# First image of a conv-attention kernel: column sums of the exp tiles taken by TensorE into a held PSUM bank, and the key maps' small levels moved to another buffer and convolved first

## The chip, the cores and the metric

The kernel runs on one core of one Trainium2 chip. The metric is the device time of one launch in microseconds (us), in float32 throughout. Three runs of the kernel before took 3240.96, 3236.12 and 3240.89 us; the median is 3240.89 us. One further execution was taken by the hardware profiler; its own time stands in the table below.

## The reference, cut to what matters

Input `x` is 8 images of 256 channels and 32x32 pixels. The network is a convolutional attention layer, then a token attention layer, then eight gated experts. Only the first layer is touched.

```python
# layer 0, per image; C = 256, HEADS = 8, DH = 32
q = einsum('bchw,oc->bohw', x, q_w)                    # 1024 queries per head
k_map, v_map = kv[:, :C], kv[:, C:]                    # kv = kv_w applied to x
def pooled(t):                                         # four levels: 32x32, 16x16, 11x11, 5x5
    for i, r in enumerate([1, 2, 3, 6]):
        p = average_pool(t, r)
        p = p + depthwise3x3(p, dconv_w[i], dconv_b[i])
        outs.append(p.reshape(B, C, -1))
    return concatenate(outs, axis=2)                   # 1024 + 256 + 121 + 25 = 1426 keys
ks_ = layernorm(pooled(k_map).T); vs_ = layernorm(pooled(v_map).T)
attn = softmax(einsum('bhqd,bhkd->bhqk', q, k) * SCALE)   # over the 1426 keys
out_att = einsum('bhqk,bhkd->bhqd', attn, v)
```

The softmax needs, for every head and query, the sum of the exponentials over all 1426 keys.

## The kernel before, in words

**Stages.** `attention` (line 913) computes layer 0 and layer 1 of all images, interleaved; `experts` follows. The main loop of `attention` walks over images b, head groups c (four heads each), halves of the queries, and key chunks kc of 128 keys. One (b, c, half) is called a unit here; a unit has 11 full chunks, and image 0 has units 0 to 3. The chunks of a unit come in the order 0 to 7, then 11 (once per image), then 8 to 10.

**One step of the loop.** `scores` (1509) makes four products with 32 contracted rows each into one tile `sc` of four PSUM banks; ScalarE takes the exponential of the tile into `pt` (128 x 2048, six buffers). One step later `values` (1519) multiplies the four heads' parts of `pt` with the value tokens `vt` into the bank `pv`. Chunk 11 has only 18 keys: `tail_scores` (1531) puts its exponentials, for all four units of an image, into the tile `ptail`, which is allocated at line 1083 and not used before that.

**The sums.** Every second exp tile is added into the one before it by an accumulating DMA that GpSimd issues (`add`, 1564), so a unit yields six "pairs"; the sixth also gets its rows of `ptail` (`tail_add`, 1556). The generator `sums` (1571) then adds pairs 1 to 5 into pair 0 on VectorE, two instructions of 128 x 1024 each, ten a unit, and at the end sums pair 0 over its partitions by four products with a block of ones. `normalise` (1590) takes the reciprocal and scales the attention output.

**PSUM.** A partition has eight banks: four for `sc`, one for `pv`, two for `sm` and one for `sx`. `small()` (929) hands out one of the last three for all work beside the loop.

**The maps of image 0.** `first_maps` (1172) projects the four maps (0 and 1 keys, 2 and 3 values) and copies them out of PSUM; the key maps' copies `p` lie in two of the six `pt` buffers, the value maps' copies in `p0` and `p1`. The 32x32 level of the keys is convolved on TensorE (`first_keys`, 1220), all other levels by `taps` (1243), eight multiply-adds on VectorE per level and map. `first_taps` (1257) does the values' large level, then the small levels of maps 2, 3, 0, 1 in this order. The small keys of map 0 are the buffer `kn`, those of map 1 the buffer `v`, the values `acc`. `key_tokens` (1473) and `value_tokens` (1460) turn finished maps into normalised tokens, in three groups of four chunks; the third group needs the small levels.

**What sets the order.** Every instruction goes through class `Flow`, whose helper at line 670 records it: so all lines of the profile say L670. `Flow` keeps its own estimate of each engine's time and lays down one fixed order for each engine. Side work is a set of generators with ranks, which yield what they need next; between two steps of the loop `step` (882) resumes those that `runnable` (855) lets through. A TensorE request is let through only if its data are expected 1.5 us before the next scores may start, and only against a credit for each step. `finish(cond)` (895) resumes generators until the condition holds, whatever the loop would do next. The loop calls it, among others, before the fifth step of image 0 (line 1917), where it waits until the small levels of both key maps are done, and before the values products of a chunk whose group of `vt` is not there (line 1934). On the chip each engine then works its order off and waits on semaphores.

**Side work named below.** `mix` and `weights1` prepare the weights of the output projection and of layer 1 (tiles `gw`, `bnvec`, `res`, `p`); `convolve` (1270) does image 1 onwards.

Of the kernel before, what the change touches and what calls it, by code (L numbers as in the profile page):

```python
# [10 lines left out]
AF = mybir.ActivationFunctionType  # L11
# [5 lines left out]
P = 128  # L17
C = 256
HW = 1024
HEADS = 8  # L20
DH = 32
# [3 lines left out]
NKC = 12  # L25
# [11 lines left out]
NEAR = {"DVE": 1.5, "ACT": 2.0, "POOL": 1.0, "SP": 10.0}  # L37
BUFS = {"sm": 2, "sx": 1}
AHEAD3 = 3
PACE2 = 8.0  # L40
NBOUND = 64
NSTAGED = 64
# [870 lines left out]
def attention(tc, kit, f, outer, ended, nb, consts, x, t1, t2, hn, bounds, vecs, q_t, kv_t, proj_t, gqk_t, wqk, wqkv, vecs1, w1_d, w1c, gate_d, wrc, vecs2, bnvec):  # L913
# [6 lines left out]
    with ExitStack() as ctx:  # L920
        l1, shared = outer
        wp = ctx.enter_context(tc.tile_pool(name="w0", bufs=1))
        work = ctx.enter_context(tc.tile_pool(name="work0", bufs=1))
        psum = ctx.enter_context(tc.tile_pool(name="psum0", bufs=1, space=PSUM))

        def T(pool, shape, tag, bufs=1):
            return f.tile(pool, shape, tag, bufs=bufs)
# [51 lines left out]
        hi, lo = bounds  # L979
        for t in bounds:  # L980
            f.pool.memset(t, 0.0)
        column = [4 * (n // 4 * 2) + n % 4 for n in range(4 * nb)]
# [98 lines left out]

        ks, qs, vts = {}, {}, {}
        ptail = T(work, [P, 4, 512], "ptail")
        vz = [T(work, [P, P], f"vz{i}") for i in range(2)]
        for t in vz:
            f.pool.memset(t, 0.0)
# [2 lines left out]
        todo, done, read, freed, key_parts, normalised = [], [], [2], [0], [0], [0]  # L1089

        def pe(*tiles, tag=None):
            return "PE", tiles, tag
# [13 lines left out]
        def until(cond):  # L1106
            return None, cond, None
# [50 lines left out]
        first, large, whole, pooled, asked = {}, [], [], [], []  # L1158
# [13 lines left out]
        def first_maps(xp):  # L1172


            for m in range(4):
                if m < 2:
                    p = T(work, [P, 4, 512], "pt", bufs=6).rearrange("p j q -> p (j q)")
                    acc = T(l1, [P, NK], "v") if m else T(work, [P, NK], "kn", bufs=3)
                else:
                    p = pmaps[m - 2]  # L1180
                    acc = T(work, [P, NK], "acc", bufs=3)
                for t in (p, acc):
                    if t is not p or m < 2:
                        f.split(t, 512, HW)
                first[m] = p, acc
            for m, s0 in [(m, s0) for g in (0, 2) for s0 in (0, 512) for m in (g, g + 1)] + [(m, HW) for m in range(4)]:
                if s0 == HW:
                    yield until(lambda: pooled)
                w = min(512, NK - s0)
                c = m % 2  # L1190
                p, acc = first[m]
                src = source(xp, s0, w)
                yield pe(src, tag="sm")
                ps = small()
                for k in range(2):
                    f.pe.matmul(
                        ps[:, :w],
                        lhsT=kvw[:, k, m * P : (m + 1) * P],
                        rhs=src[:, k, :],
                        start=k == 0,  # L1200
                        stop=k == 1,
                    )
                f.act.activation(p[:, s0 : s0 + w], ps[:, :w], AF.Copy)
                for s, n in enumerate(SIDES):
                    a, z = max(OFFS[s], s0), min(OFFS[s] + n * n, s0 + w)
                    if a < z and (m >= 2 or s):
                        f.act.activation(
                            acc[:, a:z],
                            ps[:, a - s0 : z - s0],
                            AF.Identity,  # L1210
                            bias=db(c, s),
                            scale=mid[:, c * 4 + s : c * 4 + s + 1],
                        )
                if (m, s0) == (3, 512):
                    large.append("maps")
                    f.spawn(first_keys(0), 1)
                    f.spawn(first_keys(1), 5)
            whole.append("maps")
# [21 lines left out]
                f.act.activation(acc[:, half * 512 : half * 512 + 512], ps, AF.Identity, bias=db(m, 0))  # L1240
            large.append(("keys", half))

        def taps(c, s, p, acc):
            n, o = SIDES[s], OFFS[s]
            pin = p[:, o : o + n * n].rearrange("p (h w) -> p h w", h=n)
            pout = acc[:, o : o + n * n].rearrange("p (h w) -> p h w", h=n)
            for tap in range(9):
                if tap == 4:
                    continue
                dy, dx, y0, y1, x0, x1 = windows(tap, n)  # L1250
                o_ap = pout[:, y0:y1, x0:x1]
                yield ve(pin[:, y0 + dy : y1 + dy, x0 + dx : x1 + dx], o_ap)
                f.ve.scalar_tensor_tensor(
                    o_ap, pin[:, y0 + dy : y1 + dy, x0 + dx : x1 + dx], dw(c, s, tap), o_ap, ALU.mult, ALU.add
                )

        def first_taps():
            for m in (2, 3):
                yield until(lambda: "maps" in large)
                yield from taps(m - 2, 0, *first[m])  # L1260
                large.append(("values", m))
                read[0] += 1
            yield until(lambda: whole)
            for m in (2, 3, 0, 1):
                for s in range(1, 4):
                    yield from taps(m % 2, s, *first[m])
                whole.append(m)
            done.extend(first[m][1] for m in (2, 3, 0, 1))

# [300 lines left out]

        def sums(n, pairs):

            for i in range(1, NKC // 2):
                yield until(lambda: len(pairs) > i)
                for j in range(0, 4, 2):
                    s = pairs[0][:, j : j + 2, :]
                    yield ve(s, pairs[i])
                    f.ve.tensor_tensor(s, s, pairs[i][:, j : j + 2, :], ALU.add)
            yield until(lambda: normalised[0] == n)
            yield pe(pairs[0], tag="sm")  # L1580
            total = small()
            for j in range(4):
                f.pe.matmul(
                    total[DH * j : DH * j + DH, :], lhsT=kit.ones[:, :DH], rhs=pairs[0][:, j, :], start=True, stop=True
                )
            rec = T(work, [P, 512], "rec")
            f.act.activation(rec, total, AF.Copy, accum_out=hi[:, column[n] : column[n] + 1])
            return rec
# [315 lines left out]
        for i in range(len(steps) + 1):  # L1904
            if i < len(steps):
                b, c, half, kc = steps[i]
                sl = slice(half * 512, half * 512 + 512)
                if kc % 4 == 0:
                    f.finish(lambda: key_parts[0] > 3 * b + kc // 4)
                if (half, kc) == (0, 0):  # L1910
                    f.finish(lambda: (b, c) in qs and (b or (c, 0) in asked))
                    turn[0] = 2 * b + c
                    atts[b, c] = T(work, [P, HW], "att", bufs=2)
                if kc == NKC // 2 and b < nb - 1:
                    f.sp.dma_start(t1[b][:, c, sl], x[b, c * P : (c + 1) * P, sl])
                if i == 4:
                    f.finish(lambda: {0, 1}.issubset(whole))
                if b == 0 and kc == 0:
                    f.finish(lambda: (c, half) in asked)
                if kc == NKC - 1:  # L1920
                    f.finish(lambda: key_parts[0] > 3 * b + 2 and (b, 1) in qs and (b or len(asked) == 4))
                    tail_scores(b)
                else:
                    pts[i] = scores(b, c, sl, kc)
                f.step()
            if i and steps[i - 1][3] < NKC - 1:
                b1, c1, half1, kc1 = steps[i - 1]
                if kc1 == 0:
                    pv = T(psum, [P, 512], "pv")
                    pairs = []  # L1930
                    sl1 = slice(half1 * 512, half1 * 512 + 512)
                    f.spawn(unit(b1, c1, sl1, units, pairs), 0)
                    units += 1
                f.finish(lambda: kc1 // 4 in vts[b1])
                values(b1, c1, kc1, pts[i - 1], pv)
                if kc1 % 2:
                    add(kc1, pts.pop(i - 1), pts[i - 2])
                    pairs.append(pts.pop(i - 2))
                if kc1 == NKC - 2:
                    u = 2 * c1 + half1  # L1940
                    tail_values(b1, u, pv)
                    pairs.append(pts.pop(i - 1))
                    tail_add(u, pairs[-1])
                    f.finish(lambda: projected[0] >= b1)
                    f.act.activation(atts[b1, c1][:, sl1], pv, AF.Copy)
            if i < len(steps):
                f.step((PACE, PACE1))
# [687 lines left out]
```

## Time and profile before

| what | us or share |
|---|---|
| median of three runs | 3240.89 |
| the profiled execution's own time | 3236.82 |
| its span, first to last instruction | 3235.0 |
| mean granted TensorE clock | 0.989 |
| busy: PE (TensorE matmul) | 3064.9, 95% |
| busy: DVE (VectorE) | 2458.7, 76% |
| busy: ACT (ScalarE) | 1692.2, 52% |
| busy: POOL (GpSimd) | 1198.6, 37% |
| ends of image 0's four units (copy of `pv`) | at 185.4, 224.9, 268.5, 311.8 |
| ends of image 1's first two units | at 374.9, 414.3 |
| end of the last unit | at 1856.7 |

Times of the table's last three rows are from the start of the span. A row of the profile's timeline gives start, duration, engine, line, operation, output and inputs, shapes, and in brackets how long the engine had been idle before and which instruction released it. TensorE's rows count two records for each float32 product with 32 columns or rows. PE is short for TensorE, PEclk for the clock that it was granted.

### The profile page before, as it was taken

The numbers are of one execution on the slowest core, as the hardware profiler recorded it, in microseconds if no ns is written. First come the engines' busy times: TensorE is split into PE (matmuls) and PEld (weight loads), VectorE is DVE, ScalarE is ACT, GpSimd is POOL, SyncE is SP. The second block draws the span as 40 slices with busy tenths as digits, with TensorE's granted clock in tenths as the row PEclk, the third lists the DMA queues.
The fourth block names the chain that finished last, engine by engine and source line by source line (L and its number), as shares of the span: only waits on it lengthen the run. The fifth ranks groups of instructions, "written<-read, shape, count | busy, mean of one in ns | idle before, by whom it ended". The sixth has DMA issues, their size and how long they took to land.

```text
span 3235.0 us, 55827 instructions
## 1 busy us (share of the span) xinstructions
PE 3064.9 (95%) x22342; PEld 1793.5 (55%) x22342; DVE 2458.7 (76%) x4064; ACT 1692.2 (52%) x2302; POOL 1198.6 (37%) x1293
## 2 busy tenths in 40 slices
PE   8787899999999999989999999999999999999998
PEld 3422234334334334333433367777888888888887
DVE  5787787987898889988754546346888788777776
ACT  3476676576657666676665523334333333444443
POOL 2312314214232232241111210006756666777775
PEclk9799999999999999999999999999999999999999
DMA  1277656665665565764676653124444442000000
GB/s 51 72 157 169 133 115 146 142 138 122 132 152 121 128 144 120 172 144 88 152 161 128 154 205 134 55 90 163 150 143 150 150 163 72 20 30 23 20 14 21
DMA packets 117196, 375.49 MB, mean 116 GB/s; under 512 B 14512, under 2 KB 40440, under 8 KB 93696
## 3 DMA queue, kind: packets, MB, share of 16 engines
q0 software_dynamic: 28608, 179.85, 28.7%
q1 hardware_dynamic: 84960, 190.01, 17.3%
q8 instruction: 178, 2.92, 0.4%
q10 hardware_dynamic: 3360, 1.97, 0.2%
q14 instruction: 90, 0.74, 0.1%
HBM read 118.74 MB, written 87.60 MB: 64 GB/s over the span
## 4 chain that ended last, share of the span: by engine, by line
PE 71%; DVE 10%; ACT 7%; DMA 4%; issue 4%; POOL 2%; ACTq 0%; DVEq 0%; POOLq 0%; SPq 0%
PE bank L670 22%; PE sm L670 17%; PE y L670 10%; PE sc L670 8%; PE sx L670 8%; PE pv L670 6%; ACT pt L670 5%; DMA pt<-pt 3%; DVE acc L670 3%; DVE rec L670 1%; DVE pt L670 1%; DVE h L670 1%; DMA pt<-ptail 1%; DVE c L670 1%; DVE u L670 1%
## 5 line engine op out<-in xcount | busy, mean ns | idle before, releaser
L670 ACT ACTIVATE pt<-sc 128x2048 f32<-128x2048 f32 x352 | 660.7, 1877 | 269.3 <-PE sc L670 226.8
L670 DVE SCALAR_TENSOR_TENSOR acc<-p,vec,acc 128x961 f32<-128x961 f32 (+3 forms) x960 | 554.9, 586 | 32.0 <-ACT acc L670 6.4
L670 PE MATMUL sc<-q,kn 32*128 32x512 f32 (+1 forms) x3072 | 417.3, 644 | 102.0 <-ACT pt L670 97.9
L670 DVE TENSOR_TENSOR pt<-pt,pt 128x1024 f32<-128x1024 f32 x320 | 388.1, 1260 | 125.6 <-DMA pt<-pt 110.4
L670 PE MATMUL pv<-pt,vt 128*32 128x512 f32 x2816 | 380.1, 612 | 0.1
L670 ACT ACTIVATE p1c<-bank 128x256 f32<-128x256 f32 x226 | 86.6, 383 | 556.2 <-PE bank L670 550.2
L670 ACT ACTIVATE h<-h,bnvec 128x512 f32<-128x512 f32 x452 | 341.9, 805 | 62.7 <-DVE h L670 52.6
L670 POOL DMA_DIRECT2D pt<-pt x160 | 146.1, 913 | 561.2 <-ACT pt L670 438.5
L670 POOL TENSOR_TENSOR rstd<-rstd,mhalf 128x4 f32<-128x4 f32 (+2 forms) x88 | 107.5, 1222 | 624.1 <-DVE rstd L670 592.4
L670 DVE TENSOR_TENSOR h<-p1c,bank 128x512 f32<-128x512 f32 x226 | 154.1, 682 | 222.9 <-PE bank L670 216.0
L670 PEld LDWEIGHTS sc<-q,kn 32*128 32x128 f32 (+1 forms) x3072 | 113.6, 178 | 293.4 <-ACT pt L670 195.8
L670 POOL TENSOR_TENSOR tm<-h,tm 128x256 f32<-128x256 f32 x202 | 234.7, 1162 | 15.8
L670 DVE TENSOR_TENSOR h<-u,bank 128x256 f32<-128x256 f32 x452 | 230.2, 550 | 7.8
L670 PEld LDWEIGHTS pv<-pt,vt 128*32 128x32 f32 x2816 | 55.6, 108 | 271.8 <-issue 257.1
L670 PE MATMUL bank<-h,w2e 128*128 128x256 f32 (+1 forms) x620 | 203.6, 457 | 2.8 <-DVE h L670 1.9
L670 POOL TENSOR_TENSOR tm<-h 128x512 f32<-128x512 f32 x101 | 131.8, 1304 | 189.6 <-ACT h L670 189.6
L670 DVE TENSOR_TENSOR h<-h,gate 128x1024 f32<-128x1024 f32 x128 | 199.6, 1560 | 0.5 <-ACT h L670 0.5
L670 PE MATMUL y<-t,s3e 128*128 128x256 f32 x768 | 187.0, 379 | 1.9 <-POOL t L670 1.7
L670 PE MATMUL bank<-t,s1e 128*128 128x256 f32 x750 | 182.5, 379 | 0.2 <-DVE h L670 0.2
L670 POOL TENSOR_TENSOR t<-h 128x512 f32<-128x512 f32 x104 | 135.0, 1298 | 110.3 <-DVE h L670 93.3
L670 PE MATMUL sm<-y,t 128*32 128x256 f32 (+1 forms) x1976 | 175.6, 379 | 0.1
L670 DVE TENSOR_TENSOR u<-h,bank 128x512 f32<-128x512 f32 x226 | 155.5, 688 | 24.7 <-DVE h L670 0.9
(315 smaller groups left out, 5551.8 us busy)
## 6 DMA issues: line engine op xcount, KB each, us to landing
pt<-pt POOLq DMA_DIRECT2D x160, 1024.0 KB, 7.8
h<-h SPq DMA_DIRECT2D x142, 512.0 KB
xi<-in_x_dram SPq DMA_DIRECT2D x16, 512.0 KB
t<-t SPq DMA_DIRECT2D x8, 1024.0 KB
res<-t SPq DMA_DIRECT2D x32, 256.0 KB
t<-res SPq DMA_DIRECT2D x32, 256.0 KB
hn<-res SPq DMA_DIRECT2D x32, 256.0 KB
hn<-hn SPq DMA_DIRECT2D x16, 512.0 KB
```

The source lines that it names most:

```text
L670: ins = fn(*args, **kwargs)
```

## The change

Two things change, both in image 0 alone. First, units 0 to 3 no longer add pairs on VectorE: as each pair is there, four products with ones sum it over its partitions into one `sx` bank, which stays allocated from the unit's first pair to its sixth. Second, the small levels of the two key maps are copied to `ptail`, not to the `pt` buffers that hold the maps' large levels; their taps go before those of the value maps, and the wait before the fifth step goes.

```diff
+SUMMED = 4
         ptail = T(work, [P, 4, 512], "ptail")
+        f.split(ptail, 512)
...
-                f.act.activation(p[:, s0 : s0 + w], ps[:, :w], AF.Copy)
+                small_levels = s0 == HW and m < 2
+                f.act.activation(ptail[:, m, :w] if small_levels else p[:, s0 : s0 + w], ps[:, :w], AF.Copy)
...
-        def taps(c, s, p, acc):
+        def taps(c, s, p, acc, base=0):
             n, o = SIDES[s], OFFS[s]
-            pin = p[:, o : o + n * n].rearrange("p (h w) -> p h w", h=n)
+            pin = p[:, o - base : o - base + n * n].rearrange("p (h w) -> p h w", h=n)
...
-            for m in (2, 3, 0, 1):
+            for m in (0, 1, 2, 3):
+                p, acc = first[m]
                 for s in range(1, 4):
-                    yield from taps(m % 2, s, *first[m])
+                    yield from taps(m % 2, s, *((ptail[:, m, :], acc, HW) if m < 2 else (p, acc)))
                 whole.append(m)
...
         def sums(n, pairs):
+            if n < SUMMED:
+                yield until(lambda: normalised[0] == n)
+                total = None
+                for i in range(NKC // 2):
+                    yield until(lambda: len(pairs) > i)
+                    yield pe(pairs[i], tag=None if i else "sx")
+                    if i == 0:
+                        total = T(psum, [P, 512], "sx")
+                    for j in range(4):
+                        f.pe.matmul(
+                            total[DH * j : DH * j + DH, :],
+                            lhsT=kit.ones[:, :DH],
+                            rhs=pairs[i][:, j, :],
+                            start=i == 0,
+                            stop=i == NKC // 2 - 1,
+                        )
+                rec = T(work, [P, 512], "rec")
+                f.act.activation(rec, total, AF.Copy, accum_out=hi[:, column[n] : column[n] + 1])
+                return rec
...
-                if i == 4:
-                    f.finish(lambda: {0, 1}.issubset(whole))
```

## The prediction

> **What bounds the kernel now.** I read the slices first, to see where TensorE is not full; then windows cut at the ends of units; then the timeline inside the worst window; then the waits.
>
> ```profile
> PE   8787899999999999989999999999999999999998
> DVE  5787787987898889988754546346888788777776
> PEclk9799999999999999999999999999999999999999
> ```
>
> A slice is 81 us. TensorE is at nine tenths from the sixth slice on: from there the kernel lasts as long as TensorE's work does, and whatever is gained earlier stays gained. The first five slices hold image 0. The only low clock is in the second.
>
> ```profile
> 98.80:144.00 45.20, 28.77 (x86) 20.30 (x86) 32.23 (x107) 8.25 (x18) 12.02 (x12) 0.72 0.24 63
> 144.00:185.40 41.40, 38.84 (x385) 12.93 (x384) 32.90 (x59) 32.66 (x42) 4.96 (x5) 0.98 0.60 138
> 185.40:311.80 126.40, 102.85 (x838) 29.84 (x839) 107.37 (x185) 88.62 (x92) 21.98 (x29) 0.97 0.79 174
> 311.80:374.90 63.10, 53.81 (x440) 15.91 (x443) 45.19 (x78) 45.00 (x59) 28.28 (x34) 0.97 0.64 129
> 374.90:414.30 39.40, 32.00 (x244) 8.38 (x240) 36.53 (x48) 24.11 (x21) 9.61 (x9) 0.96 0.69 137
> 414.30:760.00 345.70, 329.66 (x3452) 131.58 (x3456) 290.83 (x533) 227.13 (x286) 82.27 (x99) 1.00 0.61 133
> ```
>
> Columns: window, length, busy PE, weight loads, DVE, ACT, POOL, granted clock, DMA share, GB/s. TensorE's idle time from 98.8 to 414.3 is 16.4 + 2.6 + 23.5 + 9.3 + 7.4 = 59.2 us. In the first window it was also slow.
>
> ```profile
> 95.48 1.88 ACT L670 ACTIVATE pt<-sc 128x2048 f32<-128x2048 f32 x1 [0.46 <-PE sc L670]
> ...
> 146.06 1.88 ACT L670 ACTIVATE pt<-sc 128x2048 f32<-128x2048 f32 x1 [1.29 <-PE sc L670]
> ```
>
> ```profile
> 103.59 1.95 DVE L670 SCALAR_TENSOR_TENSOR kn<-pt,vec,kn 128x225 f32<-128x225 f32 x4
> 119.60 4.24 DVE L670 SCALAR_TENSOR_TENSOR kn<-pt,vec,kn 128x225 f32<-128x225 f32 x11
> 132.42 3.05 POOL L670 TENSOR_TENSOR bnvec<-bnvec,mhalf 128x16 f32<-128x16 f32 x1 [23.59 <-DVE bnvec L670]
> 139.88 2.15 DVE L670 SCALAR_TENSOR_TENSOR v<-pt,vec,v 128x225 f32<-128x225 f32 x6
> ```
>
> No exponential for 50 us: the loop stands before its fifth step, because VectorE does the key maps' small levels (`kn`, `v`) last and mixes them with `mix` and `weights1`.
>
> ```profile
> 193.38 1.07 PE L670 MATMUL pv<-pt,vt 128*32 128x512 f32 x8
> 194.26 1.04 PE L670 MATMUL sm<-pt,con 128*32 128x512 f32 x8
> 195.44 1.14 PE L670 MATMUL sc<-q,kn 32*128 32x512 f32 x8
> ...
> 198.58 1.14 PE L670 MATMUL sc<-q,kn 32*128 32x512 f32 x8 [1.00 <-ACT pt L670]
> ```
>
> Steps are 3.14 us apart with or without a group of ones-products: without one TensorE idles 1.00 us for the exponential, since there is one `sc` tile.
>
> ```profile
> PE sc L670 <- ACT pt L670: 40.0, 33, 3.3
> ...
> DVE pt L670 <- DMA pt<-pt: 16.5, 8, 6.1
> ```
>
> ```profile
> L670 DVE TENSOR_TENSOR pt<-pt,pt x59: 1206/1219/2676, 154.1 to 419.1; 128x1024 f32<-128x1024 f32 x59
> ```
>
> These are from 80 to 420 us: TensorE waits 33 times for the exponential; VectorE's adds, 1.22 us in the median, waited 16.5 us for accumulating DMAs.
>
> **What the Trainium skill says.** "TensorE: Matmul & The Clock Gate", Part 1: the array's clock is halved after an idle window of about 3.4 us. The trace agrees: 0.72 granted from 98.8 to 144. "PSUM — Partial Sum Buffer", section Engine vs sequencer instructions: the queues of VectorE, ScalarE and GpSimd are first in, first out, and products start in program order; so a sum waiting on TensorE holds the scores behind it. Before, the 20 later pairs waited on VectorE. "TensorEngine Tiling (Array Packing)", Key Properties: a change of tiling mode drains the array. The sums have the mode of `pv`, 128x32, and follow it above at 0.88 us; I add nothing.
>
> **The change, part by part.** Prices on TensorE, from the timeline: 0.23 us for a product of 512 columns in a 32-wide tile (so 0.92 for four), 0.27 for one of `sc`, 0.85 for a full 512-column one, 0.13 for a transpose.
>
> *Sums.* Out: 40 adds on VectorE, 40 x 1.22 = 49 us. In: 80 products, five more groups a unit in four units: 20 x 0.92 = 18.4 us on TensorE. The built order of both programs has the same work otherwise on all five queues, beside the names of banks and of the tap sources; POOL and SP keep their counts.
>
> *Small levels.* The same 96 taps, 24 a map, and copies of the same size into another buffer: nothing. The two `pt` buffers of the key maps come free after the large level (77 us in the trace) instead of at 145: this is what lets the fifth and sixth exponential start.
>
> *The wait that goes, and the one that is late next.* In the built order steps 5 to 8, the tail scores and the scores of chunks 8 and 9 now come before any wait for the values' small levels; then the values product of chunk 8 needs the third group of `vt`, which is last. So the wait moves six scores and five values products further. When does it end? VectorE has the same taps before it, less the parts of `weights1` that now come later: their instructions between 117 and 140 are some 4.8 us, and the waits for them 8.6 (5.8 for `bnvec`, 1.4 each for `gm` and `mtb`). Before, the last tap ended at 145.2; now 145.2 - 13.4 = 132. From last tap to normalised tokens the same group took 7.6 us before (taps done 103.6, ScalarE's four scalings end at 111.2), so 140; two TensorE pieces of `weights1` that stand ahead in the order make it 142. TensorE's work by then, at the prices: six scores 6.5, tail 1.6, five values 4.6, four sums 3.7, transposes 3.1, projections of image 1 5.1, `mix` and `weights1` 5.1: 29.7 us, against 15.6 in the window before. The 45.2 us window lost 29.6 us to idling and half clock; some 14 of it is recovered.
>
> *From there to unit 4.* To the end of unit 1 the order has 11 us of TensorE work: 154, against 185.4. I summed TensorE's work up to each end of a unit in both orders:
>
> | end of unit | before, us of work | after, us of work | before, measured end |
> |---|---|---|---|
> | 1 (image 0) | 125.6 | 112.9 | 185.4 |
> | 4 | 221.3 | 241.6 | 311.8 |
> | 5 (image 1) | 274.9 | 295.5 | 374.9 |
> | 6 | 304.2 | 322.4 | 414.3 |
> | 12 | 635.8 | 658.4 | 759.8 |
> | 32 | 1694.7 | 1714.0 | 1856.7 |
>
> Units 2 to 4 have 128.7 us of work now (95.7 before). Busy time ran 5 to 7% above these prices there (102.85 for 95.7); I take 135, and 10 for idling, against 23.5 before, because 17 groups of sums lie where the loop had 1.00 us of nothing. So unit 4 ends at 154 + 145 = 299, 13 us earlier with 20 us more work done. This hiding ends where a step already has a projection beside it: there a sum costs its 0.92.
>
> *Image 1.* Unit 5 took 63.1 us for 53.6 of work: VectorE was still convolving image 1 and adding pairs, and key tokens were late. Without 49 us of adds VectorE has them done first; 53.9 plus 4, ending at 357. Unit 6 has 11 steps of 3.14 at least, say 37: 394, against 414.3. Units 7 to 12: 336 of work, idle 12 where it was 16: 742, against 759.8, so 18 ahead, with 22.6 us more work behind it, of which 3.3 are paid back by the end (19.3 more in all). From there both are full: 18 + 3 = 21 us gained.
>
> Against the profiled execution's own 3236.8 (span 3235.0 and 1.8 around it) that is 3216. The median stands 4 above that execution, and the result will be a median: 3240.9 - 21 = 3220.
>
> **Unknown costs.** (a) A wait of TensorE for an accumulating DMA: no row shows it for later pairs. Below nothing is excluded, since it can only hold. At least 0, as a request is let through only when data are expected 1.5 us early; at most the 2.1 us mean of VectorE's eight waits, for 24 groups 50 us. I take 0.2 each, inside the idling above. (b) `sx` held for four units leaves two banks for side work: from 0, if two suffice, to 10 us, if a tenth of image 0's side work stalls; I take 0, since deferred work only moves to later steps. A gain is excluded. (c) Idling left in units 2 to 4: from 3 to 23.5, I take 10. (d) The layout of later images shifts by chance: the work differs by up to 9 us at single units, so plus or minus 6.
>
> **The rivals.**
> *The full relief.* VectorE is the bound of image 0 (85% busy from 185 to 312), and once relieved TensorE idles a third of 59.2 only, and half clock goes: 39 + 13 - 18.4 = 34 less, near 3205. For it: the first window. Against it: the wait comes back at chunk 8.
> *Nothing gained.* The moved wait ends as late as the old, at 150, and sums lie beside projections, so 18.4 us are paid in full: -20 + 18.4, near 3239. Against it: 33 idle gaps of 1 us.
> *Slower.* TensorE waits in order for pairs whose DMA is late. Place: the 24 groups of units 1 to 4. Gross gain is 21 + 18.4 = 39, so it decides above 39 / 24 = 1.6 us per group; at 2.1 the time is 50 - 39 = 11 above, 3252. For it: 5 us waits of `DVE pt` on the DMA, with DMA share 0.79. Against it: sums may be laid down later than the adds were.
> That the change does nothing is excluded by the counts.
>
> **How the numbers follow.** A difference above 0.2% (6.5 us) can be told from no change here. Forecast 0.50 (own range 3207 to 3232); full relief 0.22; nothing gained 0.13, of which 0.02 counts as faster and 0.01 as slower; slower 0.15, of which 0.02 within 0.2%. So faster 0.74, same 0.12, slower 0.14. The range runs from 3198, full relief less (d), to 3244: nothing gained plus (d); the far part of slower is left out.
>
> **What would show it.** In the trace after: exponentials continuing past 98 us, and a gap of about 25 us near chunk 8 instead; unit 1 ending near 154, unit 4 near 299, unit 6 near 394; 40 fewer adds. Waits of `PE sx` on `DMA pt<-pt` near zero. It is wrong if unit 4 ends after 312, or if those waits pass 20 us, or if the lead at unit 12 is gone at the last unit.

## The result, and the profile after

The kernel after took 3258.86 us (median of five runs, 3253.37 to 3261.02) beside 3240.89 us for the kernel before (3236.12 to 3246.19). The ratio is 1.0053, interval 1.0042 to 1.0065: 18 us slower, where 21 us less were forecast. The profiled execution took 3253.37 us, its span is 3251.3; that is 16.3 us over the span before.

The slices of the page of the kernel after:

```profile
PE   8888899999989989999999999999999999999998
DVE  5873888898888897888654645446878788777776
PEclk9999999999999999999999999999999999999999
```

The sevens in TensorE's second and fourth slices and the clock of 7 under the second have gone: image 0 is better. Further right TensorE's row had one eight before, in the nineteenth slice, between the sixth and the last; now it has two, in the twelfth and the fifteenth. To size this, both spans are cut at the same five places: the ends of unit 1, unit 6 (the second of image 1), unit 12 (the last of image 2) and unit 32. First the kernel before, then the kernel after; columns as in the prediction (window, length, busy PE, weight loads, DVE, ACT, POOL, granted clock, DMA share, GB/s).

```profile
0.00:185.43 185.43, 147.41 (x736) 72.12 (x736) 127.22 (x309) 89.94 (x148) 47.99 (x70) 0.91 0.28 72
185.43:414.25 228.82, 188.58 (x1513) 54.06 (x1513) 189.02 (x310) 157.69 (x169) 59.79 (x71) 0.97 0.73 155
414.25:759.83 345.58, 329.54 (x3448) 131.52 (x3452) 290.88 (x533) 227.01 (x285) 82.15 (x98) 1.00 0.61 133
759.83:1856.69 1096.86, 1046.95 (x10691) 413.30 (x10684) 870.48 (x1482) 710.80 (x858) 283.10 (x327) 1.00 0.64 137
1856.69:3235.00 1378.31, 1352.43 (x5964) 1122.49 (x5964) 981.14 (x1432) 506.79 (x844) 725.53 (x731) 0.99 0.27 95
```

```profile
0.00:150.31 150.31, 124.94 (x632) 53.95 (x636) 108.27 (x269) 81.99 (x133) 41.43 (x68) 0.95 0.29 72
150.31:403.42 253.11, 218.90 (x1853) 68.21 (x1846) 161.16 (x319) 165.96 (x185) 61.95 (x76) 0.95 0.70 150
403.42:764.69 361.27, 338.82 (x3288) 137.28 (x3292) 309.54 (x549) 235.34 (x299) 97.54 (x116) 0.98 0.57 127
764.69:1877.19 1112.50, 1049.10 (x10853) 409.66 (x10849) 855.57 (x1458) 703.69 (x843) 260.24 (x306) 0.99 0.63 135
1877.19:3251.30 1374.11, 1350.87 (x5964) 1122.90 (x5964) 981.51 (x1432) 506.52 (x844) 728.44 (x731) 1.00 0.28 95
```

Up to unit 6 the kernel after is 10.8 us ahead: TensorE's idle time fell by 18.7 us (78.3 to 59.6), its busy time rose by 7.9. From unit 6 to the end it loses 27.1 us: 17.3 of idle time (91.8 to 109.1) and 9.9 of busy time. By the built orders TensorE's side work still to come at unit 6 is the same in both within 0.2 us (18.2 more is done, of which 18.4 are the sums), so those 9.9 us are the same work at a lower clock (0.98 and 0.99 up to unit 32, where it was 1.00). Nothing that the change touches is computed there: its last instruction belongs to unit 4.

The waits of TensorE between unit 8 and unit 32 (total, times, longest), first before, then after, show another shape, not a much larger sum:

```profile
PE sc L670 <- ACT pt L670: 57.5, 65, 2.8
```

```profile
PE sc L671 <- ACT pt L671: 66.9, 50, 7.6
```

Before, 65 short waits of at most 2.8 us; after, 50, of which the longest takes 7.6. The longest, in the timeline of the kernel after (TensorE, then VectorE, then ScalarE):

```profile
1146.72 1.07 PE L671 MATMUL pv<-pt,vt 128*32 128x512 f32 x8
1155.41 2.09 PE L671 MATMUL sc<-q,kn 32*128 32x512 f32 x8 [7.63 <-ACT pt L671]
1157.43 1.94 PE L671 MATMUL pv<-pt,vt 128*32 128x512 f32 x8
...
1163.60 1.14 PE L671 MATMUL sc<-q,kn 32*128 32x512 f32 x8
```

```profile
1140.66 8.20 DVE L671 SCALAR_TENSOR_TENSOR acc<-p,vec,acc 128x100 f32<-128x100 f32 x11
1148.78 3.34 DVE L671 RECIPROCAL rec<-rec 128x512 f32<-128x512 f32 x1
1152.15 0.69 DVE L671 TENSOR_TENSOR att<-att,rec 128x512 f32<-128x512 f32 x1
```

```profile
1152.88 0.63 ACT L671 ACTIVATE rec<-rec 128x512 f32<-128x512 f32 x1 [7.66 <-DVE att L671]
...
1153.51 1.86 ACT L671 ACTIVATE pt<-sc 128x2048 f32<-128x2048 f32 x1
```

Read from below: the next exponential starts at 1153.51 because ScalarE's queue has an instruction of `normalise` ahead of it, which waited 7.66 us for VectorE's `att`; VectorE had the reciprocal laid behind eleven taps (8.20 us). And then TensorE is slow: the next scores take 2.09 us, not 1.14, and the values 1.94, not 1.07; the scores after them, 8 us later, take 1.14 again. So one badly placed reciprocal costs twice, once as idle time and once as half clock. In the kernel before the same reciprocal of that stretch (at 1141.67) stands behind a single tap of 1.21 us, and no such wait exists.

### The profile page after: what moved, and what is told of

It is laid out like the page before. It is cut to its first block, busy times and chain, and to the rows that moved or that the text cites. A ratio compares the mean times of both kernels' runs of the same rounds, so it can differ in the third digit from the quotient of the medians.

```text
span 3251.3 us, 56208 instructions
## 1 busy us (share of the span) xinstructions
PE 3082.6 (95%) x22580; PEld 1792.0 (55%) x22580; DVE 2416.1 (74%) x4024; ACT 1693.5 (52%) x2302; POOL 1189.6 (37%) x1293
## 3 DMA queue, kind: packets, MB, share of 16 engines
q1 hardware_dynamic: 84960, 190.01, 17.3%
## 4 chain that ended last, share of the span: by engine, by line
PE 67%; DVE 7%; issue 6%; DMA 4%; ACT 4%; POOL 4%; POOLq 0%; DVEq 0%; ACTq 0%; SPq 0%
PE bank L671 21%; PE sm L671 15%; PE y L671 10%; PE sc L671 8%; PE sx L671 6%; PE pv L671 6%; DMA pt<-pt 4%; ACT pt L671 3%; DVE acc L671 2%; DVE h L671 1%; DVE pt L671 1%; POOL pool L671 1%; DVE rec L671 1%; DVE c L671 1%; DVE u L671 1%
## 5 line engine op out<-in xcount | busy, mean ns | idle before, releaser
L671 DVE SCALAR_TENSOR_TENSOR acc<-p,vec,acc 128x961 f32<-128x961 f32 (+3 forms) x960 | 558.4, 589 | 42.1 <-ACT acc L671 16.5
L671 PE MATMUL sc<-q,kn 32*128 32x512 f32 (+1 forms) x3072 | 424.9, 655 | 109.2 <-ACT pt L671 106.0
L671 DVE TENSOR_TENSOR pt<-pt,pt 128x1024 f32<-128x1024 f32 x280 | 340.2, 1261 | 135.9 <-DMA pt<-pt 119.4
L671 PE MATMUL pv<-pt,vt 128*32 128x512 f32 x2816 | 387.0, 622 | 0.1
L671 POOL TENSOR_TENSOR t<-h,t 128x256 f32<-128x256 f32 x208 | 165.4, 795 | 16.3
```

What stands on the lines that cost most here:

```text
L671: ins = fn(*args, **kwargs)
```

## The experiments

Four theories. **1:** the early gain is real, and is lost because the planner, once image 0 differs, lays a wholly new order for the later images, which is by chance a worse one. **2:** the lead cannot be kept, since something else paces images 1 to 5, and the 18.4 us of sums are always paid. **3:** the sums are pure cost and the small levels pure gain. **4** (formed after the first four runs): VectorE paces images 0 and 1, so that 49 us of adds less are worth more than the products cost. Differences below are ratios times 3240 us unless said otherwise.

**A barrier at image 2.** Four kernels get a barrier where image 2 begins: all side work that can run is done there, and the planner's clocks are set equal. (It is a barrier of the planner alone; on the chip an engine can still be behind.) From there on the four orders are the same on every engine (on TensorE the last 20,600 instructions of some 22,600), beside the names of banks.

```diff
+    def settle(self):
+        self.closed = False
+        while True:
+            ready = [t for t in self.threads if t[1][0] is None and t[1][1]()]
+            ready = ready or [t for t in self.threads if self.possible(t[1])]
+            if not ready:
+                break
+            self.resume(min(ready, key=lambda t: (self.start(t) if t[1][0] else 0.0, t[2])))
+        at = max(self.now.values())
...
+        self.now = dict.fromkeys(self.now, at)
...
+                if (b, c, half, kc) == (2, 0, 0, 0):
+                    f.settle()
```

The two halves of the change were tried in it too: `SUMMED = 0` in the kernel after leaves the small levels' move alone; the block under `if n < SUMMED:` put into the kernel before leaves the sums alone.

Before with the barrier:

> The kernel before, with a barrier at the start of image 2: all side work that can be done is done there, and the planner's clocks are reset, so that from there to the end the order of instructions is the same in the four runs of this set. It is the reference of the set. All theories expect the barrier itself to cost: some tens of us of TensorE work without a loop beside it, so 3250 to 3300 us. The stretch from the barrier to the end should last the same in all four within 2 us.

After with the barrier:

> The kernel after with the same barrier. Theory 1 (the early gain is real, and is lost by the new order that the planner lays for images 1 to 7): without a new later order the gain stays, so 6 to 15 us below the barrier run of the kernel before (at the end of unit 6 the kernel after had a lead of some 11 us, side work owed counted). Theory 2 (the lead cannot be kept, because something else paces images 1 to 5, and the 18.4 us of sums are always paid): 5 to 18 us above the barrier run of the kernel before.

Small levels alone:

> Small levels in ptail alone, sums as in the kernel before, with the same barrier. Theory 1: the stall before the fifth step goes, no products are added: 10 to 25 us below the barrier run of the kernel before, and at or a little above the barrier run of the kernel after if the sums hide in image 0. Theory 2: 0 to 5 us below the barrier run of the kernel before. Theory 3 (the sums are pure cost, the small levels pure gain): 18 us below the barrier run of the kernel after.

Sums alone:

> Sums by products alone, the small levels where they were, with the same barrier. Theory 1: 18.4 us of products, of which a half lies in gaps of TensorE or is paid back by a relieved VectorE: -5 to +9 us against the barrier run of the kernel before. Theories 2 and 3: the products are paid in full, 15 to 20 us above it.

Measured, five runs each, means worked out from them (standard error about 2 us each):

| with barrier | median | mean | against before with barrier |
|---|---|---|---|
| before | 3307.71 | 3309.1 | |
| after | 3312.60 | 3311.4 | +2.3 |
| small levels alone | 3308.43 | 3306.8 | -2.3 |
| sums alone | 3292.61 | 3293.4 | -15.7 |

Against the kernel before without a barrier the four ratios are 1.0219 (1.0199 to 1.0239), 1.0230 (1.0214 to 1.0247), 1.0210 (1.0193 to 1.0227) and 1.0166 (1.0149 to 1.0184): the barrier itself costs some 70 us, more than the 60 at most that were expected. The windows up to the end of unit 11, where the drained work has long been done, in the order before, after, small levels, sums:

```profile
0.00:772.05 772.05, 630.10 (x4779) 248.01 (x4780) 595.41 (x1144) 454.15 (x586) 202.47 (x251) 0.94 0.52 115
```

```profile
0.00:767.79 767.79, 643.03 (x4813) 249.36 (x4814) 550.59 (x1105) 455.18 (x586) 196.27 (x251) 0.94 0.52 116
```

```profile
0.00:765.00 765.00, 631.21 (x4743) 243.91 (x4744) 595.78 (x1145) 454.10 (x586) 202.09 (x251) 0.93 0.52 116
```

```profile
0.00:756.84 756.84, 642.60 (x5107) 249.09 (x5108) 548.43 (x1104) 453.03 (x586) 199.38 (x251) 0.94 0.53 118
```

Idle time of TensorE there (length less busy) is 141.9, 124.8, 133.8 and 114.2 us. (From unit 11 to unit 32 the same order then took 1154.0, 1157.0, 1160.6 and 1160.2 us in these single executions, a wider spread than the 2 us expected; so one profile is not good for less than some 6 us, and the means above carry the comparison.) So the sums add 12.5 to 12.9 us of busy time, and the change takes back 17.1 us of idling: 4 us net, of which the runs show nothing at the end (+2.3, with an error of about 3). In these executions unit 6 had ended at 411.9 before and at 398.4 after, 13.4 us earlier; between unit 6 and unit 11 nine of the 13 us went, 4.2 as TensorE work that was still owed (297.0 to 301.2 us busy) and 5.0 as idling. Theory 1 asked for a gain of 6 to 15 that stays, theory 2 for 5 to 18 of loss: neither came. The larger part of the loop's lead does not last; but the 18 us of loss are not there either when the later order is the same. Theory 3 is refuted: the sums alone gain most, the small levels alone gain nothing that can be told.

Where the sums alone gain is in the same traces. The first exponential of image 2, the first step behind the barrier, starts at 590.0, 584.9, 585.4 and 586.8 us (same order): the sums alone are only 3 us ahead of before there. From it to the end of unit 11 the four take 182.0, 182.9, 179.6 and 170.0 us. VectorE still has convolution taps to do at that point; this block is about as long in the first three (37.7, 36.3 and 39.9 us) and shorter in the sums alone. Before, and the sums alone:

```profile
586.62 37.70 DVE L670 SCALAR_TENSOR_TENSOR acc<-p,vec,acc 128x16 f32<-128x16 f32 x65
```

```profile
585.38 24.05 DVE L671 SCALAR_TENSOR_TENSOR acc<-p,vec,acc 128x225 f32<-128x225 f32 x49
```

TensorE waits for these taps 9.0, 10.8 and 11.2 us in the first three, and not at all in the sums alone. So most of the 15.7 us are VectorE's relief, and they show where the barrier makes TensorE wait for VectorE. The kernel after has the same 40 adds less and yet no shorter block. Up to the first exponential of image 2 VectorE has stood idle for 124.1, 166.7, 121.6 and 157.5 us: most of its relief turned into idling, in the kernel after 9 us more of it than in the sums alone.

**The halves without a barrier**, each with the later order that the planner gives it:

> The kernel before with the sums of image 0 by products alone: the small levels stay in the buffers of the large level, their taps last, and the wait before the fifth step stays. Theory 2 or 3 (sums are paid in full): 15 to 20 us slower than the kernel before. Theory 4, from the barrier runs (VectorE paces image 0 and 1, and 49 us less on it are worth more than 18.4 us of products): 5 to 20 us faster than the kernel before. Theory 1 (the order that the planner lays for the later images decides by chance): anywhere from -20 to +20.

> The kernel after with the sums of all images by VectorE: the small levels' move alone. Theory 3: 10 to 25 us faster than the kernel before. Theory 4: the stall is only moved, since VectorE has the same work; -5 to +3 us. Theory 1: anywhere from -20 to +20. This order stages twelve more pieces of the experts' weights, which may count for a few us.

Sums alone: 3244.62 us, ratio 1.0009 (1.0001 to 1.0017), 3 us over the kernel before with 80 products more. Small levels alone: 3281.76 us, ratio 1.0127 (1.0111 to 1.0142), 41 us over it. By theory 4 the second should have been within 5. Its trace shows 29 us of the difference behind unit 32, where the change has no work at all (1407.3 us for 1378.3), with one wait that the kernel before doesn't have:

```profile
PE bank L671 <- DMA hn<-hn: 11.6, 1, 11.6
```

The first item of the experts is late. This order stages twelve more pieces of expert weights, but that need not be the reason: the same wait, 11.3 us, will be met in a neighbour of the kernel before (VectorE +5), which stages as many as the kernel before. So a half that is neutral under a fixed later order comes out 41 us slower when the order is laid anew: of the four theories only 1 allows that. The three kernels with a change agree. Against the kernel before, the kernel after is at +18 us with its own later order and at +2 with the common one, the small levels alone at +41 and -2, the sums alone at +3 and -16: 16, 43 and 19 us more with the order that each gets for itself.

**Nudges.** To see what a new order alone does, the planner's estimate of one engine's clock is set ahead once, at the start of image 2. The order of images 0 and 1 stays, and the work too, beside how some products are split.

```diff
+                if (b, c, half, kc) == (2, 0, 0, 0):
+                    f.now["DVE"] += 5.0
```

The kernel before, VectorE by 5 us, ScalarE by 2, TensorE by 2, VectorE by 8:

> The kernel before, where the planner's estimate of VectorE's clock is set 5 us ahead once, at the start of image 2: the order of images 0 and 1 stays, the later one is laid anew. Theory 1: the time moves by 5 us or more against the kernel before. Theories 2 and 3: within 4 us of it.

> The kernel before, ScalarE's clock in the planner set 2 us ahead once at the start of image 2: same work, later order laid anew. Theory 1 with a favourable order before (the order of the kernel before is an uncommonly good one among its neighbours, as the run with VectorE 5 us ahead, 45 us slower, suggests): 3250 to 3290 us. Its rival (that run was an outlier, and the kernel before stands in the middle of its neighbours): 3225 to 3250 us.

> The kernel before, TensorE's clock in the planner set 2 us ahead once at the start of image 2. Theory 1 with a favourable order before: 3250 to 3290 us. Its rival: 3225 to 3250 us.

> The kernel before, VectorE's clock in the planner set 8 us ahead once at the start of image 2. Theory 1 with a favourable order before: 3250 to 3290 us, as its three neighbours (3254, 3259, 3285). Its rival, that the families differ: below 3245 us.

The kernel after, TensorE by 1.2 us, VectorE by 1, by 8, by 3:

> The kernel after, where the planner's estimate of TensorE's clock is set 1.2 us ahead once, at the start of image 2: the order of images 0 and 1 stays as it is, the later one is laid anew, the work is the same. Theory 1: the time moves by 5 us or more against the kernel after, to either side, while units 1 to 6 end within 2 us of the kernel after. Theories 2 and 3: within 4 us of the kernel after.

> The kernel after, VectorE's clock in the planner set 1 us ahead once at the start of image 2; units 1 to 6 as in the kernel after. Theory 1: the kernel after is an ordinary order, so its neighbours lie on both sides of 3259, from 3235 to 3285 us, and their mean is not above that of the neighbours of the kernel before. Theory 2 (the lead cannot be kept and the sums are paid): neighbours of the kernel after lie 15 to 20 us above those of the kernel before.

> The kernel after, VectorE's clock in the planner set 8 us ahead once at the start of image 2; units 1 to 6 as in the kernel after. Theory 1: 3235 to 3285 us, to either side of the kernel after. Theory 2: 15 to 20 us above the mean of the neighbours of the kernel before.

> The kernel after, VectorE's clock in the planner set 3 us ahead once at the start of image 2. Theory 1: 3240 to 3275 us, with the family's mean at or below that of the neighbours of the kernel before (3266). The rival that the families differ: above 3265 us.

The sums alone, VectorE by 1 us, TensorE by 2, VectorE by 3, ScalarE by 2:

> Sums by products alone, the small levels as before, VectorE's clock in the planner set 1 us ahead once at the start of image 2. If the sums alone gain some 15 us over the family of the kernel before, as in the barrier runs: 3235 to 3260 us. If they cost their 18.4 us: 3265 to 3300 us.

> Sums by products alone, TensorE's clock in the planner set 2 us ahead once at the start of image 2. If the sums alone gain: 3235 to 3260 us. If they cost their 18.4 us: 3265 to 3300 us.

> Sums by products alone, VectorE's clock in the planner set 3 us ahead once at the start of image 2. If the family lies some 15 us under the neighbours of the kernel before (mean 3269): 3235 to 3265 us, and one below 3240 would beat both kernels. If the first three were luck: above 3265 us.

> Sums by products alone, ScalarE's clock in the planner set 2 us ahead once at the start of image 2. As before: 3235 to 3265 us if the family is lower, above 3265 us if the first three were luck.

Measured; the last columns are from the profiled executions (TensorE, unit 8 to unit 32, and what follows to the span's end):

| kernel | median us | ratio to before (interval) | unit 8 to 32: length, idle, busy | behind unit 32 |
|---|---|---|---|---|
| before | 3240.89 | | 1324.3, 64.3, 1260.1 | 1378.3 |
| before, VectorE +5 | 3284.81 | 1.0137 (1.0121 to 1.0152) | 1352.0, 80.6, 1271.4 | 1395.0 |
| before, ScalarE +2 | 3258.99 | 1.0062 (1.0043 to 1.0081) | 1348.7, 73.1, 1275.7 | 1376.8 |
| before, TensorE +2 | 3254.35 | 1.0040 (1.0029 to 1.0052) | 1338.4, 71.0, 1267.5 | 1376.5 |
| before, VectorE +8 | 3276.76 | 1.0116 (1.0095 to 1.0137) | 1358.3, 89.4, 1268.9 | 1374.2 |
| after | 3258.86 | 1.0053 (1.0042 to 1.0065) | 1350.7, 75.2, 1275.5 | 1374.1 |
| after, TensorE +1.2 | 3263.13 | 1.0066 (1.0053 to 1.0080) | 1354.3, 73.9, 1280.4 | 1380.2 |
| after, VectorE +1 | 3245.18 | 1.0009 (0.9999 to 1.0019) | 1345.5, 67.6, 1277.9 | 1376.8 |
| after, VectorE +3 | 3248.79 | 1.0029 (1.0018 to 1.0040) | 1348.0, 70.4, 1277.7 | 1378.0 |
| after, VectorE +8 | 3270.04 | 1.0089 (1.0070 to 1.0109) | 1371.1, 78.6, 1292.6 | 1371.2 |
| sums alone | 3244.62 | 1.0009 (1.0001 to 1.0017) | 1321.2, 69.1, 1252.1 | 1375.5 |
| sums, VectorE +1 | 3251.46 | 1.0037 (1.0024 to 1.0050) | 1325.8, 75.3, 1250.5 | 1377.2 |
| sums, TensorE +2 | 3249.68 | 1.0033 (1.0024 to 1.0041) | 1321.5, 68.3, 1253.2 | 1376.2 |
| sums, VectorE +3 | 3253.51 | 1.0049 (1.0032 to 1.0066) | 1303.8, 63.4, 1240.4 | 1394.3 |
| sums, ScalarE +2 | 3250.63 | 1.0035 (1.0022 to 1.0049) | 1330.7, 74.5, 1256.1 | 1380.9 |

The ratios are to runs of the kernel before on the same chip. Every neighbour of the kernel before is slower than it, by 13 to 44 us. Two of them in windows from unit 8 to unit 32, after the kernel before:

```profile
532.36:1856.69 1324.33, 1260.05 (x12785) 497.44 (x12786) 1060.80 (x1832) 860.39 (x1044) 335.05 (x388) 1.00 0.63 136
```

```profile
532.06:1880.78 1348.72, 1275.66 (x12671) 505.28 (x12672) 1055.56 (x1832) 862.25 (x1043) 342.25 (x388) 0.98 0.62 134
```

```profile
531.14:1889.43 1358.29, 1268.93 (x12683) 500.46 (x12683) 1060.93 (x1832) 862.03 (x1043) 325.04 (x388) 0.99 0.62 133
```

Both start level with the kernel before, within 1.3 us, and end 24 and 33 us behind, with the clock at 0.98 and 0.99, and 1.00 before. The neighbour with ScalarE +2 has, in its timeline, the same picture as the kernel after:

```profile
1134.34 1.07 PE L670 MATMUL pv<-pt,vt 128*32 128x512 f32 x8
1143.37 2.09 PE L670 MATMUL sc<-q,kn 32*128 32x512 f32 x8 [7.97 <-ACT pt L670]
1145.39 1.94 PE L670 MATMUL pv<-pt,vt 128*32 128x512 f32 x8
```

Here it was an accumulating DMA that ScalarE stood behind (8.74 us). In the kernel before no wait between unit 8 and unit 32 is longer than 2.8 us; in each of the other fourteen kernels of the table the longest is between 3.6 and 8.0 us.

The lead at unit 6 is no luck of one execution. The five kernels that share the order of the kernel before up to image 2 end unit 6 at 409.4 to 421.6 us, 414.5 in the mean, the five of the kernel after at 402.7 to 406.1, mean 404.1. At the end of unit 8 the means are 532.6 and 527.2: half of the lead is gone before image 2 begins.

So with the change absent, a new later order came with 13 to 44 us of loss, as theory 1 has it. How much of that is the order as such is not shown. A nudge also leaves the planner with an estimate that is off: ten of the twelve nudged kernels are slower than the kernel that they were made from, and the three largest nudges (5, 8 and 8 us) gave the three slowest medians of the table. The stronger evidence is the 16, 43 and 19 us above, where no kernel is nudged. It says too that the later order of the kernel before is a favourable one; the four slower neighbours alone could be chance. The kernel after is an ordinary member of its own family (3245 to 3270, it 3259). (Its neighbour with TensorE +1.2 is nearly a copy: only a stretch of TensorE's order and what hangs on it differs. It moved by 4 us, which lies between what the theories expected and decides nothing.) What this leaves for the change itself: the five members of the kernel after have a mean ratio of 1.0049, the four neighbours of the kernel before 1.0089, that is 13 us less for the kernel after (theory 2 asked for 15 to 20 more), with a standard error of about 9 us from the scatter: a gain is likely, but not shown, and the barrier runs show none. The sums alone have 1.0033, 18 us less than those neighbours with an error of 8, and the barrier runs agree (-15.7): so this half is likely a gain where the later order is an ordinary one. (With the kernel before counted among its own neighbours the 13 and 18 us become 7 and 12.) None of these kernels is below the kernel before; the two nearest (sums alone, and after with VectorE +1) are within 5 us of it. The sums alone with VectorE +3 come closest to a gain: the last unit ends at 1853.8 us, 2.9 before that of the kernel before, but it too has the late first item behind it (11 us of wait, and 1394.3 us for 1378.3).

Not tried: keeping the later order of the kernel before, instruction by instruction, behind the new image 0. That would need the same side work to be left at the seam.

## Why the prediction was wrong, point by point

**The stall** (holds). Exponentials go on past 98 us, at 100.65, 105.39, 112.87, 115.99, 123.79 and 127.92; the gap is at chunk 8, from there to 143.61. I had 25 us of gap, it was 14. Unit 1: 154 forecast, 150.3 measured.

**Units 2 to 4** (direction right, idling mis-sized). 135 busy and 10 idle forecast; 137.6 and 19.8 measured, so unit 4 ended at 307.7, not 299. This is unknown (c). The sums did fill gaps, but the same stretch has other waits now: VectorE, relieved, stood waiting.

```profile
DVE tst L671 <- ACT kt L671: 23.2, 3, 8.6
DVE rec L671 <- ACT rec L671: 22.6, 5, 9.5
...
DVE pt L671 <- DMA pt<-pt: 5.9, 4, 3.0
```

Those are the waits of VectorE from 80 to 420 us in the kernel after. The DMA line, 16.5 us before, fell by 10.6; the other two were 9.0 and 4.5. VectorE's busy time up to unit 6 fell from 316.2 to 269.4 us, its idle time rose from 98 to 134: the 49 us were taken off it and only a part was used. What TensorE waited for in units 2 to 4 was still the exponential: ten waits and 19.0 us, where it had been 17 and 19.9. The sums took many of the 1 us gaps, but the longest wait is now 6.4 us; there ScalarE had scalings of value tokens, which waited for VectorE, ahead of the exponential.

**Units 5 and 6.** 58 and 37 forecast, 55.8 and 40.0 measured: 403.4, not 394; this is the 8.7 us from unit 4 and 0.7 more.

**The step that failed** is the last one, and the premise under it that "whatever is gained earlier stays gained": "Units 7 to 12: 336 of work, idle 12 where it was 16" and "From there both are full: 18 + 3 = 21 us gained", with unknown (d), the layout of later images, at plus or minus 6. Units 7 to 12 took 361.3 us: 338.8 of busy time, as forecast within 3, but 22.5 of idling. Units 13 to 32 then took 15.6 us longer than before (13.5 of it idling), where 3.3 us less work was laid in, and what is behind unit 32 was 4.2 shorter. With 9.4 us at unit 6, 13.3 in units 7 to 12 and 14.7 from there to the end (15.6 - 4.2 + 3.3), the 37 us between -21 and +16 are whole. The sign that I had named, a lead at unit 12 that is gone at the last unit, came earlier still: at unit 12 the kernel after was already 4.9 us behind. I had taken "nine tenths busy" as "full" and a lead as something that a full engine keeps. But nine tenths left 90 us of idling after unit 6 that depends on the order, and the clock depends on how the idling is cut up. The three changed kernels give the size that (d) should have had, 16 to 43 us slower, and the nudges 13 to 44; it was one-sided here, because the order before was a favourable one. I compared the work of the two orders (equal within 9 us at every unit) and did not compare their quality, which the trace of before shows: its longest loop wait after unit 8 is 2.8 us. The order is not the whole of it: with the common later order the change still gained nothing (+2.3), so the 21 us were not there to be lost. Why the lead of 10 us at unit 6 shrinks to 5 at unit 8 stays open.

**Slips.** Image 0 ends at 311.8 us, in the fourth slice; the fifth is image 1 already. Three sums are out by a microsecond (142 + 11 given as 154, 3205 - 6 as 3198, 3239 + 6 as 3244); nothing hangs on them.

**The rivals.** The slower one named the wrong mechanism: there is no wait of `PE sx` on `DMA pt<-pt` in image 0 of the kernel after; unknown (a) is nothing. "Nothing gained" (-20 + 18.4) is what the barrier runs came to, near zero, though by another sum: -17.1 of idling and +12.9 of busy time. "The full relief" has a part in what the sums alone do there, -28 of idling, of which 11 lie behind the first exponential of image 2.

**The price of the sums** was a little high: 18.4 us forecast, 12.5 to 12.9 more busy time in the barrier runs.

**The Trainium skill.** Its clock rule ("TensorE: Matmul & The Clock Gate", Part 1: half clock after an idle window of about 3.4 us) I had used for the one stall in image 0 alone. The loop's waits bring the half clock as well, and it is a good part of the loss: 9.9 us of busy time behind unit 6. There the measurement decides over the page: waits of 1.86 to 3.3 us were enough in 39 of 85 cases (last section). "PSUM — Partial Sum Buffer", section Engine vs sequencer instructions, on queues that are first in, first out, is what the 7.66 us wait of ScalarE above shows; I had applied it to TensorE and not to the exponentials behind `normalise`.

## What to carry to other kernels

Where a planner lays the whole order from its own clock estimates, a change at the start is two changes: the one written, and a new order of everything after it. Before pricing the first, get the size of the second: lay the order anew with small nudges of the estimates, or put a common order behind the kernels that are compared. If the neighbours lie 13 to 44 us above the kernel, a gain of 20 us at the start is lost in it. And look at waits by length, not only by sum: all but one of the 60 waits above 3.3 us were paid again at or near half clock.

## What the runs showed of the hardware

The half clock comes after shorter waits than 3.4 us. Over the loops of all these traces (from 420 to 1860 us), a group of scores after a wait of TensorE took more than 1.25 us (1.14 is usual, 2.09 is half clock) in 4 of 90 cases for waits of 1.2 to 1.85 us, 15 of 40 for 1.86 to 2.5, 24 of 45 for 2.5 to 3.3 and 59 of 60 above 3.3. One case of the kernel before, in its timeline:

```profile
903.67 1.04 PE L670 MATMUL sx<-diag,con 128*32 128x512 f32 x8
907.02 2.09 PE L670 MATMUL sc<-q,kn 32*128 32x512 f32 x8 [2.31 <-ACT pt L670]
909.04 1.67 PE L670 MATMUL pv<-pt,vt 128*32 128x512 f32 x8
```

A wait of 2.31 us was enough there, while others of 2.5 us pass without it. What decides is in the same traces. The clock that they record is either full or half, and in all twenty it changes only at points of a grid with a step of 3.413 us, which the waits do not move. One stretch between two such points is called a cell here. The cells around that wait (columns as above: length, then busy TensorE first, and the granted clock third from the end):

```profile
903.49:906.91 3.42, 1.22 (x12) 0.13 (x4) 3.39 (x5) 2.42 (x3) 0.35 (x1) 1.00 1.06 244
906.91:910.32 3.41, 3.30 (x16) 0.91 (x20) 3.31 (x7) 1.15 (x2) 0.00 (x0) 0.50 0.96 197
910.32:913.73 3.41, 3.41 (x32) 0.83 (x28) 3.23 (x8) 1.64 (x3) 0.86 (x1) 1.00 0.96 223
```

And the long wait of the kernel after:

```profile
1146.15:1149.56 3.41, 1.64 (x16) 0.16 (x8) 3.34 (x4) 0.00 (x0) 3.10 (x5) 1.00 0.81 163
1149.56:1152.97 3.41, 0.00 (x0) 0.00 (x0) 3.38 (x3) 0.09 (x1) 2.00 (x4) 1.00 0.58 115
1152.97:1156.39 3.42, 0.98 (x4) 0.51 (x8) 3.42 (x6) 2.39 (x3) 0.00 (x0) 0.50 0.95 192
```

After a cell with 1.22 us of busy time the clock is half, after one with 1.64 it is still full. Over all twenty traces from 420 to 1860 us, a cell at full clock was followed by one at half in 132 of 132 cases when TensorE was busy for less than 40% of it, in 18 of 21 at 40 to 45%, in 8 of 102 at 45 to 60%, and in 1 of 7920 above. A cell at half clock was followed by one at full in none of 80 cases below 80%, in 1 of 9 at 80 to 85%, and in 158 of 173 above. So what halves the clock here is a cell with about 1.9 us of idling or more (55% of 3.413), and where a wait falls on the grid decides whether 2.3 us are enough. (Ends of products are modelled in the trace and some records can be missing, so a share may be off by a little.) Summed over windows of 5 us from unit 8 to unit 32 (busy time by one less the granted clock), the kernel before loses 4 us to it, and the other fourteen of the table 13 to 20, but for the sums alone with VectorE +3, which loses 4 as well.
